# A graph attention layer on one core: x loaded without zeros, Q's first rows earlier, one-hots of two batches, sums of sixteen tiles, and another split of the gathered columns

## The chip, the cores and the metric

The kernel runs on one core of a Trainium2 chip. Its time is the device time of one execution in microseconds; the figure compared is the median of several runs.

## What is computed

6250 nodes with 128 features, 206,250 edges (100,000 in both directions and a self-loop for each node), sorted by destination. Cut to what matters:

```python
Qh = (x @ WQ).reshape(N, 8, 16); Kh = (x @ WK).reshape(N, 8, 16); Vh = (x @ WV).reshape(N, 8, 16)
Eh = (edge_attr @ WE).reshape(-1, 8, 16)
score = einsum('ehd,ehd,ehd->eh', Kh[src], Qh[dst], Eh) / sqrt(16)
score = exp(clip(score, -5.0, 5.0))
wV = segment_sum(Vh[src] * score[:, :, None], dst, N)
Z  = segment_sum(score, dst, N)
out = layernorm(x + (wV / (Z[:, :, None] + 1e-06)).reshape(N, 128))
```

All arrays are float32, the indices int32.

## The kernel before

Edges are cut into 1612 tiles of 128 (one edge a partition), tiles into 406 batches of four (the last few are smaller).

**Head.** x comes transposed, with zeros between its columns (x value, zero, x value, ...), as one resident tile `spread` of 128 x 12,502 words in twelve loads; `xT_sb` is the view of its values. `table` makes K and V of 128 nodes by a matmul with `wkv_sb` and stores them in DRAM as `kv`, four blocks at a time, 13 groups, through two staging tiles (`kvst`). Meanwhile GpSimd gathers x's rows for the first XB = 12 batches, whose K and V are projected on the fly (`project`); all later batches gather from `kv`. After the table loop, `from_window(0)` makes the destinations relative to a window for 128 groups of eight tiles (stored in DRAM as `relD`) and counts how many lie inside; `build_q` makes Q's first blocks, each split into three bf16 terms and stored in `qs`; then `load_rel(0)` and `load_q` fetch what the first batches need. Up to batch 12 a planner orders the instructions; from there on the order is the program's own, on every engine.

**A batch.** The loop over b does, for one batch, steps of several: TensorE makes `eps` (edge features times WE) and `qps` (Q's rows spread to the edges: `onehotT` transposed times a window of Q, `stage_a`). `stage_b` on VectorE makes kq = K x qps, kqe = kq x eps, the reduction sc, the clip. ScalarE takes the exponential (`weigh`), VectorE the messages (`messages`), and `stage_c` sums them on TensorE by a matmul with `onehot`. The two one-hots are made by VectorE two batches ahead (`stage_0`, `stage_0t`), one instruction each a batch.

**Windows of sums.** Each group of eight tiles (`pair_of`) sums into a window of nodes; its first four tiles use nodes 0 to 63 of it, its last four nodes 16 to 79 (`HALF`), for which the shift matrix of `add_windows` has a break at row 64. Two groups share one PSUM tile, which ScalarE copies out (`sum`). When all windows of two blocks of 128 nodes are there, `finish` adds them on TensorE with shift matrices (`finps`), ScalarE copies the result (`fin`), and VectorE works through a layernorm whose steps are handed out one by one between others (`fill`, `norms`).

**Columns.** In 163 batches the fourth tile is not gathered by GpSimd. Its 128 columns of x are copied out of `spread` by node number (`columns`): 88 by ScalarE, in eleven runs of eight copies, 40 by VectorE, in five runs of eight, two columns to an operation (an OR of two eight-byte pieces, for which the zeros are there). Each run begins with a load of eight registers from `col_at`. TensorE then projects the columns (`project_columns`), ScalarE puts the result in place.

**Pace.** A gather is one indirect DMA of 128 rows, issued by GpSimd. A batch's first gather also waits for TensorE's `qps` of an earlier batch (`lag`, 12 batches back at first, 3 at the end), and for its buffer among twelve.

At batch 14 `from_window(1)` does the other 74 groups in one go, with its load right before it; at batch 60 and 80 the count of edges inside is closed, and a general path is taken at the end if one lay outside.

Of the kernel before, what the change touches and what calls it, by code (L numbers as in the profile page):

```python
# [20 lines left out]
B = 4  # L21
G = 4
HW = 64
HALF = 16
# [8 lines left out]
OHB = (3, 5)  # L33
# [17 lines left out]
COLP = (7, 3)  # L51
COLA = (8, 11)
COLV = (8, 5)
COLL = 8
RING = 4096
SUMS = 8
# [22 lines left out]
def pair_of(t):  # L79

    return (t // (2 * G), t // G % 2) if t < LAST else (NT, 1)


def pair_start(k):

    return (2 * k * G * N + NT // 2) // NT - DRIFT


def window_start(t):
    k, half = pair_of(t)  # L90
    return QL * P + HW if k == NT else pair_start(k) + HALF * half
# [8 lines left out]
def edge_attention(ctx: ExitStack, tc: tile.TileContext, x, xT, srcT, srcC, dstT, dstB, dst0, bnd, lo, eaT,  # L100
# [12 lines left out]
    NX = 12  # L113
    cuts = [(2 * N + 2) * i // NX for i in range(NX + 1)]
    for a, b in zip(cuts, cuts[1:]):
        nc.sync.dma_start(spread[:, a:b], xT[:, a:b])
# [11 lines left out]
    halves = [[cp.tile([P, B, P], F32, name=f"onehot{h}{i}") for i in range(OHB[h])] for h in range(2)]  # L128
# [11 lines left out]
    with ExitStack() as fast:  # L140
# [8 lines left out]
        nc.vector.tensor_scalar(shift[:HW], io_i[:HW], 0, None, op0=ALU.is_equal)  # L149
        nc.vector.tensor_scalar(shift[HW:], io_i[HW:], HALF - HW, None, op0=ALU.is_equal)  # L150
        nc.vector.tensor_scalar(ident, io_i[:, P:2 * P], 0, None, op0=ALU.is_equal)
        for h in range(2):
            for tl in halves[h]:
                nc.vector.memset(tl[:, :, HW - HW * h:P - HW * h], 0.0)
        nc.vector.tensor_copy(iota_f, io2)
        dB_sb = [ip.tile([P, WT * P], I32, name="dB_sb", bufs=1)]
        nc.scalar.dma_start(dB_sb[0][:min(P, NJ)], dstB[:min(P, NJ)])
# [17 lines left out]
        def count(rows, cl, vals, hi):  # L175

            nc.vector.tensor_scalar(cl, vals, 0.0, float(hi), op0=ALU.max, op1=ALU.min)
            nc.vector.tensor_tensor(cl, cl, vals, op=ALU.is_equal)
            nc.vector.tensor_reduce(cn[:rows, len(counts):len(counts) + 1], cl, axis=AX.X, op=ALU.add)
            counts.append(rows)  # L180

        def from_window(i):

            a, k = i * P, min(P, NJ - i * P)
            if i == len(dB_sb):
                dB_sb.append(ip.tile([P, WT * P], I32, name="dB_sb", bufs=1))
                nc.sync.dma_start(dB_sb[i][:k], dstB[a:a + k])
            d = dB_sb[i]
            w = ip.tile([P, 1], F32, name="wq0", bufs=2)
            nc.vector.tensor_tensor(w[:k], d[:k, :1], bnd_c[:k, i:i + 1], op=ALU.min)  # L190
            r = ip.tile([P, WT * P], BF16, name="relq", bufs=1)
            nc.vector.tensor_scalar(r[:k], d[:k], w[:k], None, op0=ALU.subtract)
            nc.sync.dma_start(relD[a:a + k], r[:k])
            cl = wp.tile([P, WT * P], F32, name="clq", tag="kvst", bufs=2)
            count(k, cl[:k], r[:k], QW - 1)
# [25 lines left out]
        def count_inside():  # L221

            W = 4 * 2 * D
            for a in range(0, NT, W):
                e = min(NT, a + W)
                cl = wp.tile([P, W], F32, name="cl", tag="kvst", bufs=2)[:, :e - a]
                count(P, cl, rel[:, a:e], HW - 1)
# [26 lines left out]

        def table(b0):
            st = wp.tile([P, KB, 2 * D], F32, name="kvst", bufs=2)
            blocks = range(b0, min(NB, b0 + KB))
            for b in blocks:
                n = min(P, N - b * P)
                ps = pair_bank(b, "kvacc", [P, 2 * D])  # L260
                made = nc.tensor.matmul(ps[:n], xT_sb[:, b * P:b * P + n], wkv_sb,
# [3 lines left out]
                else:  # L265
                    nc.scalar.copy(st[:n, b - b0, :], ps[:n])
            full = [b for b in blocks if (b + 1) * P <= N]
# [60 lines left out]
        def load_chunk(c):  # L328
# [3 lines left out]
            tl = ep.tile([P, CH * P], F32, name="ea")  # L332
# [14 lines left out]
        used = [0, 0]  # L347
# [3 lines left out]
        def columns(eng, b, share=1.0):  # L351
# [6 lines left out]
            while copied.get(engine, 0) < min(due, len(col_batches) * runs):  # L358
                k, j = divmod(copied.get(engine, 0), runs)
                copied[engine] = copied.get(engine, 0) + 1  # L360
                if k not in col_tiles:
                    col_tiles[k] = wp.tile([P, P], F32, name="xcol", bufs=4)
# [62 lines left out]

        def stage_0(b):
            t0, n = batches[b][0], len(batches[b])
            half = pair_of(t0)[1]
            oh = halves[half][used[half] % OHB[half]]
            used[half] += 1  # L430
            nc.vector.tensor_tensor(oh[:, :n, HW * half:HW * half + HW],  # L431
                                    iota_p[:, None, :].to_broadcast([P, n, HW]),
                                    rel[:, t0:t0 + n, None].to_broadcast([P, n, HW]), op=ALU.is_equal)
            st8[b] = oh, None

        def stage_0t(b):
            t0, n = batches[b][0], len(batches[b])
            oh = st8[b][0]
            ohT = wp.tile([QROWS, B * P], BF16, name="onehotT", bufs=AHEAD + 2)
# [3 lines left out]
            st8[b] = oh, ohT  # L443
# [39 lines left out]
        def windows(q):  # L483

            return [(k, pair_start(k) - q * P) for k in range(min(NT, LAST + 2 * G - 1) // (2 * G))
                    if -HW - HALF < pair_start(k) - q * P < P]

        def add_windows(ps, q, first, stop):

            parts = windows(q)  # L490
            for i, (k, s) in enumerate(parts):
                nc.tensor.matmul(ps, shift[:, P - s:2 * P - s], sums[k // 2][:, k % 2],  # L492
# [19 lines left out]
        def stage_c(b):  # L512
            n, g, oh, m = st8.pop(b)
            for i in range(n):
                t = batches[b][i]
                k, half = pair_of(t)
# [5 lines left out]
                u = k if final else k // 2  # L522
                first = u not in aggs
                if first:
                    aggs[u] = psA.tile([P, 2, MW], F32, name="agg")
                    if final:
                        add_windows(aggs[u][:, 0], QL, True, False)
                tail = k == NT if t == NT - 1 else pair_of(t + 1)[0] != k
                nc.tensor.matmul(aggs[u][:, 0 if final else k % 2], oh[:, i, :], m[:, i, :],  # L529
                                 start=not final and t % (2 * G) == 0, stop=tail)  # L530
                if tail and final:
                    norms.extend(pending)
                    pending.clear()
                    while norms:
                        fill()
                    norms.append(layernorm(nc, sp, aggs.pop(u)[:, :1], xbs.pop(QL), out, QL, 1, stores))
                elif tail and (k % 2 == 1 or t == LAST - 1):
                    sums[u] = sp.tile([P, 2, MW], F32, name="sum", bufs=SUMS)
                    nc.scalar.copy(sums[u][:, :k % 2 + 1], aggs.pop(u)[:, :k % 2 + 1])
                    while len(finished) < QL // 2 and all(v // 2 <= u for v, _ in windows(2 * len(finished) + 1)):  # L540
                        ready.append(len(finished))
                        finished.append(u)
# [11 lines left out]
        from_window(0)  # L554
        build_q(q_built(QLOOK + 2), True)
# [4 lines left out]
        load_rel(0)  # L560
        for j in range(QLOOK):
            load_q(j)

        def fill():
# [3 lines left out]
            elif norms and next(norms[0], None) is None:  # L568
                norms.pop(0)

        held = []
        for b in range(nbat + 3):
# [6 lines left out]
            if b < nbat:  # L579
# [8 lines left out]
                if b == 14:  # L588
                    from_window(1)
# [7 lines left out]
                columns(nc.scalar, b, 0.5)  # L597
            norms.extend(pending)
# [40 lines left out]
        while norms:  # L639
            fill()  # L640
# [156 lines left out]
```

## Time and profile before

| | |
|---|---|
| Median of 3 runs | 1867.37 us (1865.28 to 1867.83) |
| The profiled execution | 1864.63 us, span 1862.8 us |
| Granted TensorE clock, mean | 0.919 |
| Gathers from x, from kv | 48, 1401 |
| DMA | 381.63 MB, mean 205 GB/s |

The page of the profile gives for each engine its busy time, its share of the span and its count of instructions; for a group of instructions the line, engine, operation, what it writes and reads, the count, then busy time in us, the mean ns of one, and the idle time before them with what ended it. In a timeline a row is start, length, engine, line, operation, shape and count, and in brackets the idle time before it.

### The profile page before, as it was taken

The numbers are of one execution on the slowest core, as the hardware profiler recorded it, in microseconds if no ns is written. First come the engines' busy times: TensorE is split into PE (matmuls) and PEld (weight loads), VectorE is DVE, ScalarE is ACT, GpSimd is POOL, SyncE is SP. The second block draws the span as 40 slices with busy tenths as digits, with TensorE's granted clock in tenths as the row PEclk, the third lists the DMA queues.
The fourth block names the chain that finished last, engine by engine and source line by source line (L and its number), as shares of the span: only waits on it lengthen the run. The fifth ranks groups of instructions, "written<-read, shape, count | busy, mean of one in ns | idle before, by whom it ended". The sixth has DMA issues, their size and how long they took to land.

```text
span 1862.8 us, 48831 instructions
## 1 busy us (share of the span) xinstructions
PE 1331.3 (71%) x9376; PEld 1163.7 (62%) x9376; DVE 1679.4 (90%) x6911; ACT 1623.1 (87%) x15506; POOL 1379.9 (74%) x1456
## 2 busy tenths in 40 slices
PE   4787777677776777676777776777767767677676
PEld 3576666666675666565666665666656656666665
DVE  3479999999999999999999999998999899998997
ACT  1236999899999999999999999999899999998993
POOL 6577777777777777777777777777777777777774
PEclk8898999899989998999999999898899899888998
DMA  9767757767777587677667667667766676667662
GB/s 316 220 196 213 219 179 209 207 201 207 207 215 208 180 241 199 184 217 228 192 209 228 190 191 225 203 185 214 219 203 186 195 231 191 195 192 227 207 195 70
DMA packets 171087, 381.63 MB, mean 205 GB/s; under 512 B 58478, under 2 KB 84412, under 8 KB 170774
## 3 DMA queue, kind: packets, MB, share of 16 engines
q0 software_dynamic: 68768, 186.80, 34.2%
q1 hardware_dynamic: 100866, 190.58, 33.7%
q14 instruction: 237, 1.94, 0.3%
q8 instruction: 76, 1.25, 0.3%
q10 hardware_dynamic: 1140, 1.06, 0.2%
HBM read 363.50 MB, written 14.81 MB: 203 GB/s over the span
## 4 chain that ended last, share of the span: by engine, by line
DVE 49%; PE 15%; DMA 12%; issue 6%; DVEq 6%; POOL 3%; ACT 0%; POOLq 0%
DMA kvrows<-kv,src 12%; DVE kqe L466 9%; DVE kq L463 9%; DVE xcol L371 8%; PE eps L453 6%; DVE sc L469 6%; DVE msg L507 5%; DVEq L364 5%; DVE onehot L431 5%; DVE onehotT L441 4%; PE agg L529 4%; POOL kvrows L401 3%; PE finps L492 3%; DVE sc L472 2%; PE qps L456 1%
## 5 line engine op out<-in xcount | busy, mean ns | idle before, releaser
L401 POOL DMA_INDIRECT kvrows<-kv,src x1401 | 1333.3, 952 | 441.9 <-issue 315.5
L374 ACT COPY xcol<-xT_sb 128x4 uint8 x14344 | 1442.7, 191 | 39.9 <-issue 33.9
L453 PE MATMUL eps<-we_sb,ea 128*128 128x128 f32 x3224 | 493.0, 300 | 446.5 <-issue 224.1
L453 PEld LDWEIGHTS eps<-we_sb,ea 128*128 128x128 f32 x3224 | 429.9, 206 | 538.6 <-issue 449.1
L529 PE MATMUL agg<-msg,onehot 128*128 128x136 f32 x3224 | 536.3, 314 | 34.0 <-DVE msg L507 23.2
L529 PEld LDWEIGHTS agg<-msg,onehot 128*128 128x128 f32 x3224 | 457.0, 212 | 86.1 <-DVE msg L507 83.5
L371 DVE TENSOR_TENSOR xcol<-xT_sb 128x8 uint8 x3260 | 301.8, 160 | 24.8 <-issue 22.2
L463 DVE TENSOR_TENSOR kq<-kvrows,qps 128x512 f32<-128x512 f32 x406 | 274.5, 676 | 51.0 <-DMA kvrows<-kv,src 26.7
L507 DVE TENSOR_TENSOR msg<-kvrows,exp_p 128x512 f32<-128x512 f32 x406 | 272.1, 670 | 4.0 <-ACT exp_p L480 4.0
L466 DVE TENSOR_TENSOR kqe<-kq,eps 128x512 f32<-128x512 f32 x406 | 272.9, 672 | 1.2 <-PE eps L453 0.8
L469 DVE TENSOR_REDUCE sc<-kqe 128x32 f32<-128x512 f32 x406 | 271.1, 668 | 0.2
L456 PE MATMUL qps<-qw,onehotT 126*128 126x128 bf16 x1612 | 169.6, 230 | 0.4 <-DVE kq L463 0.4
L431 DVE TENSOR_TENSOR onehot<-iota_p,dst_sb 128x256 f32<-128x256 f32 x406 | 167.4, 413 | 0.4 <-PE agg L529 0.4
L441 DVE TENSOR_SCALAR onehotT<-relb,node 126x512 bf16<-126x512 bf16 x406 | 148.3, 366 | 5.3 <-PE qps L456 2.7
L479 ACT ACTIVATE msg<-sc 128x32 f32<-128x32 f32 x406 | 92.9, 229 | 65.5 <-DVE sc L472 61.6
L456 PEld LDWEIGHTS <-onehotT 126*128 126x128 bf16 x1612 | 135.2, 104 | 9.4 <-issue 0.6
L383 PE MATMUL colkv<-wkv_sb,xcol 128*128 128x256 f32 x326 | 108.7, 418 | 0.0
L472 DVE TENSOR_SCALAR sc<-sc 128x32 f32<-128x32 f32 x406 | 84.5, 208 | 0.4
L492 PE MATMUL finps<-sum,shift 128*128 128x136 f32 x640 | 80.0, 282 | 0.0
L492 PEld LDWEIGHTS finps<-sum,shift 128*128 128x128 f32 x640 | 76.5, 191 | 0.0
L480 ACT ACTIVATE exp_p<-sc 128x32 f32<-128x32 f32 x406 | 74.1, 183 | 0.0
L401 POOL DMA_INDIRECT kvrows<-x,src x48 | 45.7, 952 | 21.2 <-issue 11.9
(73 smaller groups left out, 553.4 us busy)
## 6 DMA issues: line engine op xcount, KB each, us to landing
ea<-eaT SPq DMA_DIRECT2D x201, 512.0 KB
relb<-relD SPq DMA_DIRECT2D x100, 504.0 KB
kvrows<-kv,src POOLq DMA_INDIRECT x1401
qw<-qs SPq DMA_DIRECT2D x202, 31.5 KB
kv<-kvst SPq DMA_DIRECT2D x12, 512.0 KB
xT_sb<-xT SPq DMA_DIRECT2D x10, 521.0 KB
qs<-qst SPq DMA_DIRECT2D x48, 96.0 KB
xb<-x SPq DMA_DIRECT2D x24, 128.0 KB
```

What stands on the lines that cost most here:

```text
L371: eng.tensor_tensor(to[:, 4 * (j + c):4 * (j + c) + 8], *both, op=ALU.bitwise_or)
L374: copy(to[:, 4 * (j + c):4 * (j + c) + 4], xT_bytes[:, ds(at[c] - XT_AT, 4)])
L401: ins = nc.gpsimd.indirect_dma_start(out=g[:k, i, :f], out_offset=None, in_=rows, in_offset=bass.IndirectOffsetOnAxis(ap=src_col(t)[:k], a ...
L431: nc.vector.tensor_tensor(oh[:, :n, HW * half:HW * half + HW], iota_p[:, None, :].to_broadcast([P, n, HW]), rel[:, t0:t0 + n, None].to_bro ...
L441: nc.vector.tensor_scalar(ohT[:, :n * P], rels[t0 // RC][:, e0:e0 + n * P], node[:QROWS], None, op0=ALU.is_equal)
L453: nc.tensor.matmul(pe[:, i, :], ea[:, i * P:i * P + P], we_sb, start=True, stop=True)
L456: expanded[b] = nc.tensor.matmul(pq[:, i, :], ohT[:, i * P:i * P + P], loaded[t0 // WT], start=True, stop=True)
L463: nc.vector.tensor_tensor(t0[:, :n], g[:, :n, :D], pq[:, :n], op=ALU.mult)
L466: nc.vector.tensor_tensor(t1[:, :n], t0[:, :n], pe[:, :n], op=ALU.mult)
L469: nc.vector.tensor_reduce(sc[:, :n], t1[:, :n].rearrange("p b (h d) -> p b h d", h=H), axis=AX.X, op=ALU.add)
L507: nc.vector.tensor_tensor(m[:, :n, :D].rearrange("p b (h d) -> p b h d", h=H), g[:, :n, D:].rearrange("p b (h d) -> p b h d", h=H), exp_p[ ...
L529: nc.tensor.matmul(aggs[u][:, 0 if final else k % 2], oh[:, i, :], m[:, i, :], start=not final and t % (2 * G) == 0, stop=tail)
```

## The change

- x comes without zeros (128 x 6250). VectorE writes the zeros into `spread`. A group of four blocks is loaded into a staging tile (four groups ahead, `stage_x`), used by the table's matmuls from there, and copied into `spread` by ScalarE.
- The first three steps of `from_window(0)`, `build_q`, `load_rel(0)` and the three `load_q` move into the table loop, after its second group.
- The counting becomes a generator: its remaining steps and all of `from_window(1)` come one a batch from batch 30 on; its destinations are loaded into a slot of the ring of edge chunks.
- `stage_0` and `stage_0t` make the one-hots of two batches by one instruction each.
- A window of sums takes sixteen tiles (four quarters, 16 nodes apart, 112 nodes in all) in place of eight. The one-hot's place in its tile does the shift inside a window, so the sum is one 128 x 136 tile and the shift matrix is a plain one.
- Column tiles: 167 in place of 163; 80 columns by ScalarE (ten runs), 48 by VectorE (six runs), five buffers.
- At the end the layernorm steps between the last batches are held back, and those left are handed out in turn with the last block's.

```diff
-HALF = 16
+QUAD = 4
+STEPS = 16
-OHB = (3, 5)
+OHB = 5
-COLP = (7, 3)
-COLA = (8, 11)
-COLV = (8, 5)
+COLP = (16, 7)
+COLA = (8, 10)
+COLV = (8, 6)
-SUMS = 8
+SUMS = 9
...
+def window_of(t):
+    return (t // (QUAD * G), STEPS * (t // G % QUAD)) if t < LAST else (NT, HW)
+def first_node(k):
+    return (QUAD * k * G * N + NT // 2) // NT - DRIFT
...
-    for a, b in zip(cuts, cuts[1:]):
-        nc.sync.dma_start(spread[:, a:b], xT[:, a:b])
+    nc.vector.memset(spread.rearrange("p (n z) -> p n z", z=2)[:, :, 0], 0.0)
+    nc.vector.memset(spread[:, 2 * N + 1:], 0.0)
...
+        def stage_x(b0):
+            if b0 >= NB:
+                return
+            n = min(KB * P, N - b0 * P)
+            staged[b0] = wp.tile([P, KB * P], F32, name="xst", tag=("kq", "kqe")[b0 // KB % 2], bufs=2)
+            nc.sync.dma_start(staged[b0][:, :n], xT[:, b0 * P:b0 * P + n])
         def table(b0):
+            rows, width = staged.pop(b0), min(KB * P, N - b0 * P)
+            nc.scalar.copy(xT_sb[:, b0 * P:b0 * P + width], rows[:, :width])
...
+            stage_x(b0 + 4 * KB)
...
         def stage_0(b):
+            group = together(b)
+            if not group:
+                return
+            t0, n = batches[b][0], sum(len(batches[i]) for i in group)
+            tl = onehots[used[0] % OHB]
...
+            for i in group:
+                st8[i] = tl, HW + (batches[i][0] - t0) * P - window_of(batches[i][0])[1], None
...
-                elif tail and (k % 2 == 1 or t == LAST - 1):
-                    sums[u] = sp.tile([P, 2, MW], F32, name="sum", bufs=SUMS)
-                    nc.scalar.copy(sums[u][:, :k % 2 + 1], aggs.pop(u)[:, :k % 2 + 1])
+                elif tail:
+                    sums[k] = sp.tile([P, MW], F32, name="sum", bufs=SUMS)
+                    nc.scalar.copy(sums[k], aggs.pop(k)[:, 0])
...
+        for b0 in range(0, 4 * KB, KB):
+            stage_x(b0)
+        counting = from_window(0)
         for b0 in range(0, NB, KB):
             made = table(b0)
+            if b0 == KB:
+                for _ in range(3):
+                    next(counting)
+                build_q(q_built(QLOOK + 2), True)
+                load_rel(0)
+                for j in range(QLOOK):
+                    load_q(j)
...
-        from_window(0)
-        build_q(q_built(QLOOK + 2), True)
+        second_half = itertools.chain(counting, from_window(1))
...
-                if b == 14:
-                    from_window(1)
+                if b >= 30:
+                    next(second_half, None)
...
+            late[:] = [False] * 9 + [True] if b >= nbat - 2 else []
...
         while norms:
-            fill()
+            for steps in list(norms):
+                if next(steps, None) is None:
+                    norms.remove(steps)
```

More of the change, by code (lines that the diff above doesn't have):

```diff
@@ L1 @@
+import itertools
 from contextlib import ExitStack
@@ L127, in edge_attention @@
     ident = cp.tile([P, P], F32, name="ident")
[L128 removed]
+    onehots = [cp.tile([P, HW + 2 * B * P], F32, name=f"onehot{i}") for i in range(OHB)]
     cnt_i = cp.tile([1, 1], I32, name="cnt_i")
@@ L567, in fill @@
                 build_q(0, False)
-            elif norms and next(norms[0], None) is None:
+            elif norms and (not late or late.pop()) and next(norms[0], None) is None:
                 norms.pop(0)
-        held = []
+        held, late = [], []
         for b in range(nbat + 3):
```

112 lines of the change are left out of this document (52 added, 60 removed).

## The prediction

> **What bounds the kernel now.** I read the page first, then busy time by stretches, the waits by stretches, and the timelines of the head, of one iteration and of the end.
>
> ```profile
> span 1862.8 us, 48831 instructions
> ...
> PE 1331.3 (71%) x9376; PEld 1163.7 (62%) x9376; DVE 1679.4 (90%) x6911; ACT 1623.1 (87%) x15506; POOL 1379.9 (74%) x1456
> ...
> L401 POOL DMA_INDIRECT kvrows<-kv,src x1401 | 1333.3, 952 | 441.9 <-issue 315.5
> ...
> L371 DVE TENSOR_TENSOR xcol<-xT_sb 128x8 uint8 x3260 | 301.8, 160 | 24.8 <-issue 22.2
> ...
> L492 PE MATMUL finps<-sum,shift 128*128 128x136 f32 x640 | 80.0, 282 | 0.0
> ```
>
> The profiled execution took 1864.63 us, 1.8 us more than its span and 2.7 us less than the median of the runs (1867.37 us). I make the sum against 1864.63. VectorE is the busiest, but GpSimd's 74% misleads: a gather is 952 ns busy, and the idle time before it waits for nothing ("issue"). The stretches show it.
>
> ```profile
> 212.00:1114.00 902.00, 650.36 (x4718) 568.50 (x4717) 858.04 (x3612) 862.11 (x8403) 683.26 (x719) 0.94 0.70 207
> ```
>
> The columns are PE, PEld, DVE, ACT, POOL. In 902 us GpSimd ran 719 gathers, one every 1.2545 us, without a pause: it is a full engine. The same two stretches for the line of kq alone, one per batch, and what VectorE waited for in each:
>
> ```profile
> 212.00:1114.00 902.00, 141.34 (x208) 0.94 0.70 207
> 1200.00:1800.00 600.00, 91.13 (x134) 0.91 0.69 203
> ```
> ```profile
> DVE rz L727 <- ACT fin L502: 19.5, 12, 2.1
> DVE xcol L371 <- issue: 12.5, 40, 0.5
> ...
> DVE kq L463 <- DMA kvrows<-kv,src: 1.3, 3, 1.0
> ...
> DVE kq L463 <- DMA kvrows<-kv,src: 20.5, 9, 3.0
> ```
>
> The first three waits are of 212 to 1114 us, the last of 1200 to 1800. In the first stretch a batch took 902/208 = 4.34 us with almost no wait for gathered rows: the gathers had a lead, and VectorE set the pace alone. In the second a batch took 600/134 = 4.48 us, and VectorE lost 20.5 us waiting for rows: the lead was used up and GpSimd set the pace. So two paths end nearly together. The gathers' path is full from the first gather of kv to the last; VectorE's has about 21.8 us (20.5 + 1.3) of air and no more. A gain needs both to shorten.
>
> **The head.** It sets where both paths begin.
>
> ```profile
> 0.91 2.19 DVE L154 MEMSET onehot<- 128x256 f32 x8
> ...
> 8.60 0.30 DVE L208 TENSOR_TENSOR dst_sb<-dst_sb,lo_sb 128x132 f32<-128x132 int32 x1 [5.47 <-DMA lo_sb<-lo]
> ...
> 76.78 0.69 DVE L463 TENSOR_TENSOR kq<-kvrows,qps 128x512 f32<-128x512 f32 x1 [7.68 <-PE qps L456]
> ...
> 135.79 0.16 DVE L190 TENSOR_TENSOR wq<-dB_sb,bnd_c 74x1 f32<-74x1 int32 x1 [3.51 <-DMA dB_sb<-dstB]
> ```
> ```profile
> 59.64 0.69 PE L261 MATMUL kvacc<-wkv_sb,xT_sb 128*106 128x256 f32 x2 [1.30 <-ACT kvst L266]
> ...
> 66.71 1.11 PE L416 MATMUL xtps<-ident,kvrows 128*128 128x128 f32 x4 [4.60 <-DVE qr L291]
> ```
> ```profile
> 72.32 0.59 ACT L424 COPY kvrows<-kvps 128x512 f32<-128x512 f32 x1 [1.12 <-PE kvps L423]
> ```
> ```profile
> 81.72 0.95 POOL L401 DMA_INDIRECT kvrows<-kv,src  x1 [13.21 <-DVE msg L507]
> ```
> ```profile
> 20.00:30.00 10.00, 1.84 (x4) 1.51 (x5) 0.76 (x2) 1.02 (x3) 7.54 (x8) 0.50 1.02 385
> ```
> ```profile
> xT_sb<-xT SPq DMA_DIRECT2D x10, 521.0 KB
> ```
>
> The table ends on TensorE at 60.3 us. Then Q's first rows and a count come (to 66.7), batch 0 is projected (to 72.9), and the first kq still waits until 76.8 because Q's rows must go out and come back. The first gather from kv waits 13.2 us for batch 0's messages, which free its buffer. And VectorE meets one pause of 3.5 us at 135.8 for the second window's destinations.
>
> *x without zeros.* The twelve loads of x are some 521 KB each, 6.25 MB; half of that, 3.1 MB, goes. In 20 to 30 us the DMA engines were full at 385 GB/s, so this is 8.1 us of a head that the DMA bounds. Added are 13 ScalarE copies of 128x512, 0.59 us each by the row at 72.32, in a stage where ScalarE is busy 1.0 of 10 us: nothing. VectorE writes 6251 zeros a partition: by the memset row (2.19 us for eight of 256) at most 6.7 us, where it idles 5.5 us before 8.6; the first copies of the table come a little later, under the DMA. Without that cover it would be 7.7 us on ScalarE and 1.2 us on VectorE.
>
> *Q's first rows early.* The four blocks, the broadcast load and the three window loads go into the table loop after its second group. Two pieces leave the path: 60.3 to 66.7, and 72.9 to 76.8. kq 0 then follows the table by the projection alone, 6.2 us: 60.3 - 8.1 + 6.2 = 58.4, a gain of 18.4 us. What stands against it is SP's queue: the loads of Q windows wait there for the landing of Q's stores, and the next stores of kv and the next loads of x are queued behind them. If that eats the 8.1 us, 10.3 remain; the range takes in 0. On VectorE the 20 small steps stand ahead of copies that the DMA delays anyway. GpSimd gets one thing: batch 0's messages would be done before its 48 gathers from x (now ended at 68.5), so up to 12.9 of the 13.2 us go.
>
> *Counting in steps.* The work stays; the pause of 3.5 us I take as gone (0 in the range, as the subtraction still comes right behind its load). The second window's destinations now pass through one slot of the ring of edge chunks; a chunk is loaded two ahead, so I put that at nothing.
>
> **The steady part, on VectorE's queue.**
>
> ```profile
> 700.74 0.70 DVE L371 TENSOR_TENSOR xcol<-xT_sb 128x8 uint8 x8
> 701.72 0.40 DVE L371 TENSOR_TENSOR xcol<-xT_sb 128x8 uint8 x4 [0.27 <-issue]
> 702.03 0.15 DVE L743 TENSOR_TENSOR w<-y 128x2 f32<-128x2 f32 x1
> ...
> 702.43 0.69 DVE L463 TENSOR_TENSOR kq<-kvrows,qps 128x512 f32<-128x512 f32 x1
> 703.03 0.42 DVE L431 TENSOR_TENSOR onehot<-iota_p,dst_sb 128x256 f32<-128x256 f32 x1
> 703.37 0.15 DVE L745 SCALAR_TENSOR_TENSOR y<-w,y 128x2 f32<-128x2 f32 x1
> ...
> 704.03 0.35 DVE L441 TENSOR_SCALAR onehotT<-relb,node 126x512 bf16<-126x512 bf16 x1
> 704.30 0.15 DVE L743 TENSOR_TENSOR w<-y 128x2 f32<-128x2 f32 x1
> ...
> 705.56 0.70 DVE L371 TENSOR_TENSOR xcol<-xT_sb 128x8 uint8 x8
> 706.17 0.15 DVE L744 TENSOR_TENSOR w<-w,vh 128x2 f32<-128x2 f32 x1
> ...
> 1830.05 0.28 DVE L441 TENSOR_SCALAR onehotT<-relb,node 126x256 bf16<-126x256 bf16 x1
> 1830.25 0.68 DVE L469 TENSOR_REDUCE sc<-kqe 128x32 f32<-128x512 f32 x1
> ```
> ```profile
> L364 DVEq TENSOR_LOAD <-col_at x815: 591/606/1001, 152.5 to 1822.7; - x163
> ```
> ```profile
> 312.27 3.31 PE finps L492 x28
> ```
>
> Instructions overlap, so I price each by the time from its start to the next one's start.
>
> *Columns.* A run is one load of eight registers (L364) and four operations. Runs go from 815 (3260/4) to 167 x 6 = 1002: 187 more. Per batch that is 2.14 before and 2.63 after, so iterations with three runs go from one in seven to five in eight. Two runs took 0.61 us (705.56 to 706.17), three took 1.29 (700.74 to 702.03): here the third cost 0.68, of which 0.27 is idle time while its load had not come. The mean such wait is 0.31 (12.5/40), and four operations are 0.31, so I take 0.62: 187 x 0.62 = +116 us. The ends are 0.31, with the load hidden, and 0.91, with its 606 ns wholly in the open.
> The Trainium skill (DMA: Bandwidth & Descriptors, section Latency and other measured facts) gives such a load a floor of about 600 ns, to be spread over much work, which speaks against more runs; the row's 606 ns agrees, but the 0.27 us of idle time shows over half of it covered, and by the bare floor the added runs would be 170 us and the time 1912.
>
> *One-hots of two batches.* The 256-wide one takes 0.34, a 512-wide operation of the same kind 0.60 (kq): 203 x (2 x 0.34 - 0.60) = -16 us. onehotT takes 0.27 for 512 and 0.20 for 256 (to its next start, 1830.05), so 0.07 per 256 and 0.41 at most for 1024: 203 x 0.13 = -26; since one start in place of two also halves what each now loses to delays, I take -30 (0 to -40). Nobody new waits: both are made two batches ahead as now.
>
> *Sums of sixteen tiles.* A window of 112 nodes every 62 meets a block of 128 (128+112)/62 = 3.9 times; two blocks at two passes make 15.5 matmuls in place of 640/24 = 26.7. At 3.31/28 = 0.118 us that is 1.3 us earlier for fin, for which VectorE's rz waits 1.6 each time (19.5/12): 23 x 1.3 = -30 us. The ends are 0, if TensorE's next work holds VectorE instead, and -37, the whole wait. ScalarE's sums get narrower and it has 984 fewer column copies; VectorE hardly waits for it, so that is worth nothing.
>
> *Waits for rows.* The 21.8 us above go to some 1 once the gathers are further ahead: -21. *The end.* One finish with 24 matmuls lies on it, and layernorm steps stand between its last small batches: -4 (0 to -6).
>
> Sum on VectorE's path: -18.4 - 3.5 + 116 - 16 - 30 - 30 - 21 - 4 = -6.9, which gives 1857.7, say 1858. The gathers' path: -12.9, 4 gathers fewer -5.0, the end -4: -21.9. So VectorE becomes the bound of the whole run, and it decides.
>
> **Rivals.** *GpSimd stays the bound.* If an added run costs 0.54 us or less (a quarter of the idle time hidden), VectorE's sum falls to the gathers' -21.9 and the time is 1843. For it: TensorE and ScalarE have room, and the 0.31 hidden price is seen for each second run. Against it: every row with a third run shows the idle time. *The third load costs more.* From 0.66 us a run (0.62 + 6.9/187) the change is no gain. At the row's 0.68 it gives 1869; at 0.72 it gives 1876, which I take for this case, because the wait then comes in most iterations and nothing is left to catch up in. For it: 0.68 is what the row shows; against it: the mean wait of 0.31. *The head gains less.* If SP's queue, held up by the waits for Q's rows, makes the table end at 60 us as now, 8.1 us are lost: 1866, no change.
>
> **How the numbers follow.** Forecast 0.38 (1858, own range 1851 to 1864), GpSimd the bound 0.20 (1843), dearer loads 0.28 (1876, the Trainium skill's 1912 at its far end), the head 0.14 (1866). Under 0.2% (3.7 us) a measurement of this kernel cannot tell from no change. Faster: 0.31 of the forecast, all of the first rival, 0.03 of the head: 0.54. Same: 0.07 + 0.02 + 0.06 = 0.15. Slower: 0.31. The range 1841 to 1880 leaves out the far ends of the first two rivals.
>
> **What would show it.** Right: kq 0 at about 58 us; gathers from kv starting right behind those from x; no wait of kq for rows until late; waits of xcol for "issue" grown to near 70 us; rz waiting under 0.5 us a time; fewer than 400 finps matmuls; a batch at some 4.46 us all through. Wrong: kq 0 after 66 us; kq waiting for rows through the second half (then GpSimd bounds it); onehotT over 0.5 us to its next start; or a third run that takes over 0.66 us.

## The result: slower, 1908.5 us

The changed kernel takes 1908.52 us (five runs, 1907.38 to 1916.83); the kernel before, run beside it, 1867.65 us (1865.28 to 1869.42). The ratio is 1.023, interval 1.0214 to 1.0245. In a later comparison it was 1909.3 us beside 1863.5 (1.0257, 1.0235 to 1.0279). The forecast was 1858 us and its range ended at 1880. Thirteen of the runs told below lay on three other chips, on which the kernel before takes 2529 to 2536 us, so they are read only against the kernel before on the same chip.

The page of the changed kernel's profile; the profiled execution took 1908.6 us.

```profile
span 1906.5 us, 47770 instructions
...
PE 1331.8 (70%) x9112; PEld 1172.8 (62%) x9112; DVE 1734.1 (91%) x7262; ACT 1569.7 (82%) x14539; POOL 1386.5 (73%) x1452
...
L385 DVE TENSOR_TENSOR xcol<-xT_sb 128x8 uint8 x4008 | 376.7, 160 | 67.7 <-issue 62.5
```

The span grew by 43.7 us. VectorE's busy time grew by 54.7 us, and its idle time before the columns from 24.8 to 67.7. What VectorE waited for, over the whole span (us in total, times, longest):

```profile
DVE xcol L385 <- issue: 62.5, 174, 0.6
DVE wq L187 <- DMA dB_sb<-dstB: 18.1, 2, 12.1
...
DVE rz L759 <- ACT fin L532: 11.2, 11, 2.5
...
DVE kq L493 <- DMA kvrows<-kv,src: 3.0, 5, 1.9
```

The waits for gathered rows are all but gone (3.0 us, 26.7 before): GpSimd is ahead to the end, and VectorE sets the pace alone. The stretches of before again, first the line of kq, then GpSimd's gathers:

```profile
212.00:1114.00 902.00, 134.81 (x199) 0.89 0.67 197
1200.00:1800.00 600.00, 89.64 (x133) 0.91 0.69 200
```
```profile
212.00:1114.00 902.00, 662.82 (x691) 0.89 0.67 197
```

A batch takes 902/199 = 4.53 us early and 600/133 = 4.51 late (4.34 and 4.48 before). The gathers, 719 in that stretch before, are 691: now they are held back by VectorE. Three places of the timeline:

```profile
56.59 0.68 PE L274 MATMUL kvacc<-wkv_sb,xst 128*106 128x256 f32 x2 [0.37 <-ACT kvst L279]
```
```profile
61.16 0.69 DVE L493 TENSOR_TENSOR kq<-kvrows,qps 128x512 f32<-128x512 f32 x1 [4.22 <-ACT kvrows L438]
...
213.50 0.16 DVE L187 TENSOR_TENSOR wq<-dB_sb,bnd_c 74x1 f32<-74x1 int32 x1 [12.08 <-DMA dB_sb<-dstB]
...
904.11 0.67 DVE L493 TENSOR_TENSOR kq<-kvrows,qps 128x512 f32<-128x512 f32 x1
904.82 0.69 DVE L496 TENSOR_TENSOR kqe<-kq,eps 128x512 f32<-128x512 f32 x1
905.54 0.69 DVE L499 TENSOR_REDUCE sc<-kqe 128x32 f32<-128x512 f32 x1
906.14 0.68 DVE L537 TENSOR_TENSOR msg<-kvrows,exp_p 128x512 f32<-128x512 f32 x1
...
907.89 0.40 DVE L385 TENSOR_TENSOR xcol<-xT_sb 128x8 uint8 x4 [0.43 <-issue]
...
908.29 0.68 DVE L493 TENSOR_TENSOR kq<-kvrows,qps 128x512 f32<-128x512 f32 x1
908.89 0.68 DVE L455 TENSOR_TENSOR onehot<-iota_p,dst_sb 128x512 f32<-128x512 f32 x1
909.49 0.67 DVE L496 TENSOR_TENSOR kqe<-kq,eps 128x512 f32<-128x512 f32 x1
910.09 0.48 DVE L468 TENSOR_SCALAR onehotT<-relb,node 126x1024 bf16<-126x1024 bf16 x1
910.48 0.68 DVE L499 TENSOR_REDUCE sc<-kqe 128x32 f32<-128x512 f32 x1
```
```profile
69.70 0.94 POOL L415 DMA_INDIRECT kvrows<-kv,src  x1 [0.30 <-issue]
```

The table ends at 57.3 us (60.3 before), kq 0 starts at 61.2 (76.8), and the gathers from kv follow those from x without a pause. Then there is a pause of 12.1 us for the second window's destinations (3.5 before). In the iteration, the batch at 908.29 has the merged one-hots between its steps: kq, onehot, kqe and onehotT follow one another at 0.60 us. The batch at 904.11 has nothing there: from kq to kqe it is 0.71 us, from kqe to the reduction 0.72, from the reduction to the messages, which don't need its result, 0.60. Each of the first two steps reads what the one before it writes. In the whole trace 123 kq stand right before their kqe, at a median of 0.715 us from start to start, and 128 kqe right before their reduction, at 0.722; with a one-hot behind them both take 0.60.

VectorE is one queue, so its time adds up. For the table each operation counts from its start to the next one's, less the idle time in front of the next, and idle time stands in rows of its own; a column sums to the span. The four last columns are experiments told below. rz is the first step of the layernorm, which waits for `fin`. In a second profile of the changed kernel (span 1905.1 us) the rows for the columns, their idle time, the one-hots, onehotT and the three steps come out within 1.5 us of the first.

| us | before | changed | one-hots single | columns back | load early, runs apart | all three |
|---|---|---|---|---|---|---|
| until kq 0 | 76.8 | 61.2 | 63.7 | 61.9 | 62.8 | 63.8 |
| columns | 271.7 | 345.9 | 340.9 | 274.3 | 321.6 | 261.1 |
| idle before columns | 24.8 | 67.7 | 63.3 | 27.8 | 10.8 | 7.2 |
| one-hots | 136.1 | 119.3 | 133.9 | 119.5 | 118.5 | 119.0 |
| onehotT | 113.8 | 83.7 | 115.0 | 84.2 | 82.1 | 82.8 |
| kq, kqe, reduction, and gaps under 0.15 us before the last two | 723.0 | 754.5 | 723.0 | 755.4 | 740.4 | 746.1 |
| rz for fin | 36.4 | 11.2 | 8.2 | 15.5 | 6.6 | 17.1 |
| second load of destinations | 3.5 | 12.1 | 11.5 | 12.3 | 0.0 | 0.0 |
| kq for rows from kv | 26.7 | 3.0 | 1.2 | 31.1 | 38.3 | 67.8 |
| kq for anything else | 16.6 | 10.2 | 13.7 | 30.4 | 38.6 | 45.4 |
| all else | 433.3 | 437.8 | 437.9 | 446.2 | 435.2 | 443.1 |
| span | 1862.8 | 1906.5 | 1912.4 | 1858.6 | 1854.8 | 1853.5 |

### The profile page after: what moved, and what is told of

Read it like the earlier page. It is cut to its first block, busy times and chain, and to the rows that moved or that the text cites. A ratio compares the mean times of both kernels' runs of the same rounds, so it can differ in the third digit from the quotient of the medians.

```text
span 1906.5 us, 47770 instructions
## 1 busy us (share of the span) xinstructions
PE 1331.8 (70%) x9112; PEld 1172.8 (62%) x9112; DVE 1734.1 (91%) x7262; ACT 1569.7 (82%) x14539; POOL 1386.5 (73%) x1452
## 3 DMA queue, kind: packets, MB, share of 16 engines
q0 software_dynamic: 68576, 186.28, 34.2%
## 4 chain that ended last, share of the span: by engine, by line
DVE 52%; DMA 14%; PE 12%; issue 9%; POOL 6%; DVEq 6%; ACT 1%; SPq 0%; ACTq 0%; POOLq 0%
DMA kvrows<-kv,src 11%; DVE kqe L496 10%; DVE xcol L385 9%; DVE kq L493 9%; DVE sc L499 6%; POOL kvrows L415 6%; DVE msg L537 5%; DVEq L378 5%; PE eps L483 5%; DVE onehot L455 4%; DVE onehotT L468 3%; PE agg L557 3%; DVE sc L502 2%; PE finps L522 1%; PE kvps L437 1%
## 5 line engine op out<-in xcount | busy, mean ns | idle before, releaser
L388 ACT COPY xcol<-xT_sb 128x4 uint8 x13360 | 1367.7, 190 | 95.5 <-issue 86.4
L483 PE MATMUL eps<-we_sb,ea 128*128 128x128 f32 x3224 | 510.4, 307 | 497.5 <-issue 316.6
L483 PEld LDWEIGHTS eps<-we_sb,ea 128*128 128x128 f32 x3224 | 441.9, 212 | 596.7 <-issue 527.8
L557 PE MATMUL agg<-msg,onehot 128*128 128x136 f32 x3224 | 558.6, 324 | 39.5 <-DVE msg L537 36.9
L557 PEld LDWEIGHTS agg<-msg,onehot 128*128 128x128 f32 x3224 | 479.7, 221 | 72.4 <-DVE msg L537 62.5
L385 DVE TENSOR_TENSOR xcol<-xT_sb 128x8 uint8 x4008 | 376.7, 160 | 67.7 <-issue 62.5
L455 DVE TENSOR_TENSOR onehot<-iota_p,dst_sb 128x512 f32<-128x512 f32 (+2 forms) x206 | 137.9, 670 | 2.0 <-PE agg L557 2.0
L468 DVE TENSOR_SCALAR onehotT<-relb,node 126x1024 bf16<-126x1024 bf16 (+2 forms) x206 | 101.5, 493 | 1.9 <-PE qps L486 1.4
L415 POOL DMA_INDIRECT kvrows<-x,src x48 | 45.9, 956 | 21.9 <-issue 12.5
L404 ACT COPY kvrows<-colkv 128x256 f32<-128x256 f32 x167 | 60.4, 362 | 0.8 <-PE colkv L397 0.8
L397 PEld LDWEIGHTS colkv<-wkv_sb,xcol 128*128 128x128 f32 x334 | 59.5, 219 | 2.1 <-ACT xcol L388 2.1
## 6 DMA issues: line engine op xcount, KB each, us to landing
qw<-qs SPq DMA_DIRECT2D x202, 31.5 KB
```

Of the source, the lines that this page charges most:

```text
L385: eng.tensor_tensor(to[:, 4 * (j + c):4 * (j + c) + 8], *both, op=ALU.bitwise_or)
L388: copy(to[:, 4 * (j + c):4 * (j + c) + 4], xT_bytes[:, ds(at[c] - XT_AT, 4)])
L397: nc.tensor.matmul(pk, col_tiles.pop(k), wkv_sb, start=True, stop=True)
L415: ins = nc.gpsimd.indirect_dma_start(out=g[:k, i, :f], out_offset=None, in_=rows, in_offset=bass.IndirectOffsetOnAxis(ap=src_col(t)[:k], a ...
L455: nc.vector.tensor_tensor(tl[:, HW:].rearrange("p (t n) -> p t n", n=P)[:, :n, :HW], iota_p[:, None, :].to_broadcast([P, n, HW]), rel[:, t ...
L483: nc.tensor.matmul(pe[:, i, :], ea[:, i * P:i * P + P], we_sb, start=True, stop=True)
```

## The experiments

Three things had gone otherwise than forecast by the table: the load's pause (a), the steps that stand back to back (b), and, as forecast but the largest of all, the columns (c). For each the theory is that it counts in full, because VectorE is the bound; the rival, that its time would only turn up elsewhere.

**The load early (a).** In `from_window`, behind the load:

```diff
             (nc.sync if i else nc.scalar).dma_start(d[:k], dstB[a:a + k])
+            for _ in range(4 * i):
+                yield
             w = ip.tile([P, 1], F32, name="wq0", bufs=2)
```

> The changed kernel with four empty steps between the load of the second window's destinations and its use. Theory (VectorE's queue sets the end of the whole run, so every stop of it counts): the 12.1 us for which VectorE waited for that load go, 1908.5 becomes about 1896. Rival (TensorE, whose granted clock was 0.894, or the gathers set the end): the stop is absorbed, 1908 stays.

> The changed kernel with four empty steps between the load of the second window's destinations and its use, once more, since its first run fell on a chip where the kernel before itself took 2536 us. Theory (VectorE's queue sets the end where the kernel before takes 1867 us): 12.1 us of stop go, 1.023 of before becomes 1.016, about 1896. Rival (TensorE's clock or the gathers set the end): 1908.

> The changed kernel with the second window's destinations loaded four steps of its generator ahead of their first use. Changed kernel: 1908.5 us. Theory (VectorE sets the end all through, so a stall of VectorE counts in full): the 12.1 us wait behind the load goes, 1896 us. Rival (the stall is time that VectorE would otherwise wait for gathered rows): 1908 us, with the 12 us turned up as waits for kvrows.

Measured on the three slower chips: 2458.2 us (0.9708 of before, 0.9671 to 0.9746), 2462.6 (0.9725, 0.9662 to 0.9788), 2459.1 (0.9705, 0.9666 to 0.9744). None of the numbers could be met there, and the changed kernel itself was not run there: inconclusive on the total. The pause is settled by the same edit in the table's last two columns: 0.0 where it was 12.1. That the total falls by as much is not shown, since on a chip like the first the load early ran only together with another edit.

**The load wider (a).** `dB_sb` is loaded from 128 rows in place of 74, out of a padded tensor; only the first 74 are used:

```diff
-            (nc.sync if i else nc.scalar).dma_start(d[:k], dstB[a:a + k])
+            (nc.sync if i else nc.scalar).dma_start(d, dstB[a:a + P])
```

> The changed kernel with the second load of destinations padded from 74 to 128 rows (more bytes, same place, same use). Theory: 74 rows are spread over few DMA engines (74 = 2 x 37), which is why 296 KB took over 12 us; 128 rows spread over all, so the wait falls from 12.1 to 3 to 6 us and the time to about 1900. Rival (the load stands behind others in the queue): more bytes land no earlier, the wait stays 12 us or grows, 1908 to 1910.

Measured 2466.2 us on a slower chip (0.9747 of before, 0.9709 to 0.9784): no verdict on the total. VectorE's wait for the load is 5.3 us, within the 3 to 6 of the theory; with 74 rows it was 9.4 on this chip (one-hots single, below) and 12.1 in the changed kernel. The rows of the tile show the load, here and in a kernel with the 74 rows on another slower chip (one-hots single, below); the last two numbers of a row are first and last start:

```profile
L187 DVE TENSOR_TENSOR wq<-dB_sb,bnd_c x2: 155/157/159, 19.7 to 289.9; 128x1 f32<-128x1 int32 x1, 74x1 f32<-74x1 int32 x1
...
L185 SPq DMA_DIRECT2D dB_sb<-dstB x1: 380/380/380, 281.2 to 281.2; - x1
```
```profile
L187 DVE TENSOR_TENSOR wq<-dB_sb,bnd_c x2: 156/158/159, 18.7 to 296.6; 128x1 f32<-128x1 int32 x1, 74x1 f32<-74x1 int32 x1
...
L185 SPq DMA_DIRECT2D dB_sb<-dstB x1: 257/257/257, 282.2 to 282.2; - x1
```

From issue to use it is 8.7 us with 128 rows and 14.5 us with 74 (14.5 in the changed kernel too, 199.00 to 213.50, and 13.5 with single one-hots on the chip of the wide load). More bytes arrive sooner. The DMA view shows how few engines were at work: from 290 to 296 us of the run with 74 rows the queue of this load took 10.0% of sixteen engines' time, which makes 1.6 engines; from 282 to 289 us of the run with 128 rows, where a load of edge features went beside it, 83.7%, or 13.4 engines. The Trainium skill (DMA: Bandwidth & Descriptors, section Why a DMA increments its semaphore by 16 and not by 1) says that such a load goes over the largest number of DMA engines, up to 16, that divides its number of rows on both sides; by that rule it would be 2 for 74 rows and 16 for 128. The two shares above agree with it.

**One-hots for one batch at a time (b).** The merging undone, all else as changed; ten buffers of one batch in place of five of two:

```diff
         def together(b):
-            t0 = batches[b][0]
-            n = len(batches[b])
-            if n == B and b + 1 < nbat and len(batches[b + 1]) == B and t0 % (2 * B) == 0:
-                return [b, b + 1]
-            return [] if n == B and t0 % (2 * B) else [b]
+            return [b]
```

> The changed kernel with the one-hots of one batch per instruction again (two more buffers' worth of them, all else as changed). Theory: the instructions themselves cost 47 us more (16.8 and 30.1 by the traces), but kq, kqe and the reduction, which depend on each other, are no longer back to back in every second batch and give back about 33: +14, 1922. Rival (merging is a plain gain and kq and kqe got longer for another reason, such as TensorE writing the same PSUM): the whole 47, 1955.

> The changed kernel with the one-hots of one batch per instruction, once more. Theory: +47 us of instructions, -33 us from kq, kqe and the reduction no longer standing back to back: 1922 (1.030 of before). Rival (merging is a plain gain): 1955 (1.047).

> The changed kernel with the one-hots built for one batch at a time again (400 instructions instead of 200, and as many copies of the transposed ones). Theory (the merged one-hots had covered the distance between the dependent steps kq, kqe and the reduction): one-hots +17 us and their transposed copies +30 us, kq, kqe and the gaps behind them -33 us: 1922 us. Rival (merging saves what the prediction said, 46 us, and kq and kqe are longer for another reason): 1955 us.

> The changed kernel with the one-hots built for one batch at a time again (400 instructions instead of 200, and as many copies of the transposed ones). Theory (the merged one-hots had covered the distance between the dependent steps kq, kqe and the reduction): one-hots +17 us and their transposed copies +30 us, kq, kqe and the gaps behind them -33 us: 1922 us where the kernel before takes 1865. Rival (merging saves what the prediction said, 46 us, and kq and kqe are longer for another reason): 1955 us.

> The changed kernel with the one-hots built for one batch at a time again (400 instructions instead of 200, and as many copies of the transposed ones). Theory (the merged one-hots had covered the distance between the dependent steps kq, kqe and the reduction): one-hots +17 us and their transposed copies +30 us, kq, kqe and the gaps behind them -33 us: 1922 us where the kernel before takes 1865. Rival (merging saves what the prediction said, 46 us, and kq and kqe are longer for another reason): 1955 us.

The last of these lay on a chip like the first: 1907.6 us (1903.97 to 1914.44) beside 1864.9, ratio 1.0221 (1.0199 to 1.0244). The others, on the slower chips: 2478.7 (0.977), 2466.8 (0.9734), 2473.5 (0.9767), 2479.5 (0.9812), no verdict, as the changed kernel was not run there. So merging the one-hots is worth nothing that a measurement can tell: the changed kernel's ratio of 1.023 lies in this interval, and its 1.0257 of the later comparison above it. The rival's 1955 is far off, and the theory's 1922 too high by 14. The timeline of this run, where every batch has its two one-hots between the steps:

```profile
903.74 0.68 DVE L489 TENSOR_TENSOR kq<-kvrows,qps 128x512 f32<-128x512 f32 x1
904.34 0.41 DVE L451 TENSOR_TENSOR onehot<-iota_p,dst_sb 128x256 f32<-128x256 f32 x1
904.67 0.67 DVE L492 TENSOR_TENSOR kqe<-kq,eps 128x512 f32<-128x512 f32 x1
905.27 0.50 DVE L464 TENSOR_SCALAR onehotT<-relb,node 126x512 bf16<-126x512 bf16 x1
905.69 0.67 DVE L495 TENSOR_REDUCE sc<-kqe 128x32 f32<-128x512 f32 x1
```

kq to onehot 0.60, kqe to onehotT 0.60: no step costs more than in before, and the table's row of kq, kqe and reduction is back at 723.0 us to the tenth. (On the slower chips the same row, worked out in the same way, is 730.3 to 731.2 us in the four profiles with single one-hots and 755.3 to 769.6 in the nine with merged ones.) The one-hots and their copies cost 45.9 us more than merged (248.9 against 203.0); the chain of the steps 31.5 less, the columns with their idle time 9.4 less, rz 3.0 less; the rest, head and other waits, 3.8 more. The theory had counted only the chain. (The profile here is of the slowest of the four runs, 1914.4 us, so its span stands above the median.)

**The columns in runs apart (c).** VectorE's two or three runs of an iteration stood behind one another; here up to two of them go between the steps of `stage_b`, the same columns by the same engine:

```diff
                 stage_0(b + AHEAD)
+            if b < nbat:
+                columns(nc.vector, b, 1 / 3)
             fill()
...
                 stage_0t(b + AHEAD)
+            if b < nbat:
+                columns(nc.vector, b, 2 / 3)
             fill()
```

> The changed kernel with VectorE's runs of columns spread over three places of an iteration (behind kq, behind kqe, behind the messages) in place of one; the same instructions. Theory: the register loads are then covered (62 us of idle before xcol fall under 15) and the runs stand between the dependent steps (most of 33 us): 80 us less on VectorE, so the gathers' path becomes the bound and the time lies at 1845 to 1860. Rival 1 (a load costs the queue its 0.6 us wherever it stands): no gain, 1900 to 1910. Rival 2 (TensorE bounds at its lower clock): 1890 or more.

> The changed kernel with VectorE's runs of columns spread over three places of an iteration, once more. Theory: idle before xcol from 62 to under 15 us and most of the 33 us of dependent steps gone, so the gathers' path bounds: 1845 to 1860 (0.988 to 0.996 of before). Rival 1 (a load costs 0.6 us of the queue wherever it stands): 1900 to 1910. Rival 2 (TensorE bounds): 1890 or more.

> The changed kernel with VectorE's three runs of eight columns set apart in the iteration, with other work between them, the same columns by the same engine. Theory (the third load of registers is exposed because it stands behind two others): idle before the columns 62 -> about 7 us, the columns' own time -24, the waits for gathered rows +40, so 1867 us (the earlier run with the load early as well, 1855, and the 12 us of that load). Rival (the loads cost the same wherever they stand): 1900 us or more.

Only the slower chips were met: 2437.9 us (0.9639 of before, 0.9597 to 0.9681), 2438.9 (0.9649), 2447.0 (0.9654, 0.9623 to 0.9686). It is the fastest variant of each of the three chips, and idle time of the columns for "issue" there is 4.7 us where the kernel with the early load has 123.3. On a chip like the first this edit did not run by itself, so that neither its forecasts of the total nor its rivals are settled; the next run has it together with the load early.

**Early load and runs apart, beside the changed kernel itself.**

> The changed kernel itself, as the one to hold the variants against on the chips that now run them, where the kernel before takes 2534 us and not 1868. If VectorE's queue sets the end here too, it is slower than before by about 40 us (1.015). If ScalarE's copies of columns set it, of which the change has 984 fewer, it is faster: the variant with the columns of before took 0.992 of before there and the one with the early load 0.972, so about 0.973.

> The changed kernel with both the runs spread over three places and the load four batches ahead. Where before takes 1868 us: 1840 to 1850, bounded by the gathers. Where it takes 2534 us: 2425 to 2440, as the spread alone took 2438 and the 12 us of the load are hidden there behind other stops.

On one chip: the changed kernel 1909.3 us, this one 1855.06 (1850.81 to 1858.77), beside 1863.5 of before: ratio 0.9947 (0.9928 to 0.9965). The two edits take 54 us off and make it faster than both kernels, by 0.5% against the one before. The 1840 to 1850 of the forecast was missed by 5 us. Its waits, and a stretch of its timeline:

```profile
DVE kq L495 <- DMA kvrows<-kv,src: 38.3, 28, 4.0
DVE kq L495 <- PE qps L488: 21.2, 36, 2.8
...
DVE xcol L387 <- issue: 6.5, 21, 1.4
```
```profile
908.65 0.68 DVE L495 TENSOR_TENSOR kq<-kvrows,qps 128x512 f32<-128x512 f32 x1
909.24 0.39 DVE L387 TENSOR_TENSOR xcol<-xT_sb 128x8 uint8 x4
909.56 0.67 DVE L498 TENSOR_TENSOR kqe<-kq,eps 128x512 f32<-128x512 f32 x1
910.16 0.38 DVE L387 TENSOR_TENSOR xcol<-xT_sb 128x8 uint8 x4
910.47 0.67 DVE L501 TENSOR_REDUCE sc<-kqe 128x32 f32<-128x512 f32 x1
```

A run here costs 0.32 us (909.24 to 909.56), with its load hidden behind kq, which the rival of 0.6 us wherever the load stands does not allow, and it stands where the one-hots stood, so that it covers the dependent steps as well: the row of kq, kqe and reduction falls from 754.5 to 740.4. VectorE saves 81.2 us on the columns, 14.1 on the steps and 12.1 on the load; 63.7 us come back as waits of kq: 35.3 for rows, because the gathers have become the bound (715 of them from 900 to 1800 us, one every 1.26), and 28.4 for other things, half of it TensorE's qps, whose cause was not followed up.

**The columns divided as before (c).** 88 by ScalarE, 40 by VectorE, 163 tiles:

```diff
-COLP = (16, 7)
-COLA = (8, 10)
-COLV = (8, 6)
+COLP = (7, 3)
+COLA = (8, 11)
+COLV = (8, 5)
```

> The changed kernel with the columns of before (163 tiles, 88 by ScalarE, 40 by VectorE), all else as changed. Theory: VectorE loses the 117 us that the columns added and would end near 1791, so the gathers' path bounds and the time is 1843 to 1855 (0.987 to 0.993 of before). Rival (the stop of 12 us, TensorE or ScalarE sets the end): 1880 or more.

> The changed kernel with the columns divided among the engines as before the change; all else as changed. Theory (the columns cost VectorE 117 us, all of it on the path until the gathers bound): VectorE's work falls by more than the 65 us that there are above the gathers' path, so the gathers bound: 1843 to 1855 us. Rival (what was dear is the merged one-hots and not the columns): 1880 us or more.

> The changed kernel with the columns divided among the engines as before the change; all else as changed. Theory (the columns cost VectorE 117 us, all of it on the path until the gathers bound): VectorE's work falls by more than the 65 us that there are above the gathers' path, so the gathers bound: 1843 to 1855 us. Rival (something else that the change brought holds VectorE, and the columns lie partly beside waits): 1880 us or more.

On a chip like the first: 1857.7 us (1856.08 to 1860.51) beside 1865.2, ratio 0.9956 (0.994 to 0.9973). So the new split of the columns is enough to account for the whole loss: without it the change is a gain of 7.5 us, although the load's 12 us and the chain's 31 us are still there, since the gathers now bound it. VectorE's columns and the idle time before them fall by 111.5 us and the span by 47.9; of the rest, 48.3 us is kq waiting again (for rows 3.0 to 31.1, for other things 10.2 to 30.4). The theory's upper end of 1855 was missed by 3 us. On the slower chips the same edit came out at 2514.0 us (0.9917) and 2501.0 (0.987), where the other variants beside them lay at 0.965 to 0.977: this points to a gain of 1% or more there by columns on VectorE, the opposite of here, but it is not shown, since the changed kernel itself did not run on those chips. What ScalarE and VectorE wait for on such a chip (load early):

```profile
ACT xcol L390 <- issue: 522.9, 993, 1.2
...
DVE msg L539 <- ACT exp_p L512: 134.9, 68, 4.7
```

ScalarE's copies stand idle 523 us for nothing that the profile shows (86.4 us in the changed kernel on the first chip), and VectorE waits for ScalarE's exponential. Why these chips do that is not known.

**All three.** Early load, runs apart and the columns divided as before:

> The changed kernel with the load of destinations early, VectorE's runs of columns apart and the columns divided as before the change. Theory (the gathers set the end as soon as VectorE's pace is under 4.48 us a batch): no better than k1 by more than 6 us, 1843 to 1852 us, with waits for kvrows in the place of what VectorE saves. Rival (VectorE's stalls still count, 12 us of the load and about 15 us of exposed register loads): 25 us or more below k1.

1855.25 us (1852.73 to 1855.46) beside 1865.2, ratio 0.9942 (0.9925 to 0.9958), 2.4 us below the kernel with only the columns back, where the rival wanted 25; the theory's upper end was missed by 3 us again. GpSimd's gathers in two thirds of the span:

```profile
600.00:1800.00 1200.00, 909.35 (x955) 0.89 0.69 202
```

One gather every 1200/955 = 1.2565 us, the pace at which GpSimd was full before (1.2545), while VectorE waits 67.8 us for rows. What VectorE saves beyond the columns is lost to that, and the version with 167 tiles (1855.06) ends at the same place.

## Why the prediction was wrong

The likeliest case said 1858 and the end on VectorE's path. The path was right, the sum on it was not. Its terms, with what they measured (VectorE's column of the table, changed less before):

- *Columns, +116.* Measured +74.2 and +42.9 of idle time: +117.1, or 0.63 us a run where 0.62 was forecast, and "issue" at 62.5 where near 70 was named. The largest term was the best, though with single one-hots the same columns cost 9.4 us less, so that a part of it belongs to the merging. That the Trainium skill's floor of 600 ns a load gave 1912, near the result, is chance: it put the loss into the columns, at 170 us.
- *One-hots and onehotT, -46: the step that failed.* The term counted what the merging takes away and put what it lays bare at nothing. Their own time fell as forecast, by 16.8 and 30.1 us. But the price was taken from the instruction alone, and "nobody new waits" was only argued for TensorE. Each one-hot had stood between two steps of which the second needs the first's result. Made for two batches at once it is missing in every other batch, and VectorE waits for itself: +31.5 us in kq, kqe and reduction. The trace of before held the price, though not in the iteration that was read: in its first batches the reduction and the clip that reads it stand side by side,

```profile
78.51 0.68 DVE L469 TENSOR_REDUCE sc<-kqe 128x32 f32<-128x512 f32 x1
79.22 0.18 DVE L472 TENSOR_SCALAR sc<-sc 128x32 f32<-128x32 f32 x1
```

0.71 us apart and not 0.60. Two such pairs in 203 batches at 0.11 us would have been 45 us, the whole gain, as a bound; where a layernorm step comes to stand in between, less. The 251 pairs of the changed kernel, at some 0.12 us each, make 30 of the 31.5 us. The run with single one-hots puts the net gain at nothing that can be measured. Without these 46 us the other gains do not pay for the columns, whose cost the prediction had right.
- *The pause for the destinations, -3.5: failed too.* It was taken as gone, with 0 as the worse end; it became 12.1 us. The change takes the load into the counting, but load and first use stay in one step, at 199.00 and directly behind it, with loads of edge features and relative destinations issued just ahead (195.88 and 196.45). "Loaded two ahead" was true of the ring and not of this use of it. The end of the range should have been the whole time of such a load, 10.1 us in before (issued at 125.69, used at 135.79).
- *Sums of sixteen tiles, -30.* rz waits 25.2 us less, 370 finps matmuls: right in kind, 5 us too much, since 11 waits of 1 us remain.
- *The head, -18.4.* Measured -15.6. The table ended at 57.3 us and not at 52.2, so that x without its zeros gave 3.0 of the 8.1 us; 2.3 of the 5.1 missing came back, since batch 0's projection took 3.9 us behind the table (57.3 to 61.2) and not 6.2. What the table's copies on VectorE wait for is now above all the stores of kv, which free their staging tiles (14.0 us in all).
- *Waits for rows, -21, and the end, -4.* Measured -23.7 and -2.3 (from the eighth last kq to the end of the span, 34.2 us before and 31.9 now).

The failures are one-hots whose 46.9 us brought 15.4 on VectorE's path (31 lost), the pause (12), sums (5) and head (3): 51 us, which is what separates 1858 from 1908.6; the deviations of all other rows cancel to within 1 us. This adds up rows of the traces; only the one-hots' part was also tested by itself on the total. The rival of dearer loads had the right sign for the wrong reason: an added run cost 0.63 us, under its 0.66. The rival with GpSimd as the bound came true in the versions with the runs apart, where a run costs 0.33 us on average, its idle time included; its time of 1843 was too low by 12. In the version with all three the first gather from kv comes 10.4 us earlier (81.7 to 71.3) and the last 7.0 (1842.9 to 1835.9), with 1401 gathers as before: GpSimd's pauses between them grew by 3.4 us in all. With 1397 gathers it is no better, 70.0 to 1835.3, so that the 5.0 us for four gathers fewer did not come either; and the end, after the last gather, gave 2.3 and 0.4 us in place of 4.

## What to carry to other kernels

On an engine whose queue is the bound, an instruction between two dependent ones can be partly free, as here: before merging or moving it, look at what its two neighbours would then cost side by side, and count that for every place. A load whose latency is in the open goes between other long instructions rather than behind another load; here that, with the load early, took the changed kernel from 1909 to 1855 us with all its columns. And where a load and its use sit in one step, the stall is nearly the load's whole way (12.1 of 14.5 us here), whatever ring its buffer comes from.

## What the runs showed of the hardware

- VectorE, 128x512 f32: 0.60 us from start to start when the next instruction is independent, 0.71 to 0.72 when it reads the result (904.11 to 905.54 above; the same medians in a profile of a slower chip, load early). The Trainium skill (Vector Engine (DVE) Microarchitecture Reference, section 5.2 Measured stream behaviour on trn2) gives 1.0417 ns a column and some 75 ns an instruction, from which an estimate for 512 columns is 0.61 us; this agrees with the first figure, and the section states no price for the second.
- A load of 74 rows of 4 KB took 13.2 to 15.8 us from issue to use in the thirteen profiles of the changed kernel and its variants that use it at once, one of 128 rows 8.7 us.
- Three of the chips run the same kernel 36% slower (2530 us for 1865), with granted clocks of 0.77 to 0.79 in the variants' profiles where the others show 0.89 to 0.92, and with ScalarE's small copies idle for "issue" for over 500 us. What an edit is worth may have the other sign there, as the runs with the columns divided as before suggest.
